# A graph layer with a gate on one core: more S1 T1 products split into quarters, and the order around them

## The chip, the cores and the metric

The kernel runs on one core of a Trainium2 chip. The metric is the device time of one execution in microseconds; the runs of the kernel before gave 1323.67, 1325.24 and 1325.05, median 1325.05. The profile is one further execution, with every engine's instructions recorded.

## The reference

1250 nodes with rows of 1024, 20000 edges (sorted by destination) of 8 types; everything is f32.

```python
h = maximum(layernorm(x), 0)
u = h @ root + bias
for r in range(8):                       # mean of the messages of type r, by destination
    sums = segment_sum(h[src] * (etype == r), dst); cnt = segment_sum(etype == r, dst)
    u = u + (sums / maximum(cnt, 1)) @ weight[r]
z = concatenate([u, h], 1) @ w_gate + b_gate
out = x + tanh(u) * z + h * (1 - z)
```

So there are eleven products of a 1250 x 1024 matrix with a 1024 x 1024 one: eight with `weight[r]`, one with `root`, and two with the halves of `w_gate`.

## The kernel before, in words

**Matrices and pairs.** The matrices are numbered s = 0 to 10 (`mats`, line 670): 0 to 7 are the types, 8 is `root`, 9 the half of `w_gate` that takes h, 10 the half that takes u. The kernel multiplies h by `weight[r]` first and gathers afterwards: row d of the result of type r goes to DRAM (`y`), and the edges fetch rows of it. The ten blocks of 128 nodes are taken as five *pairs* i = 0 to 4 (block i with block i + 5; NP = 5). `step(s, i)` does one pair of one matrix by `product`. The last matrix has a loop of its own at the end of the file.

**Strassen, once and twice.** `product` multiplies a pair (256 x 1024) by the matrix as 2 x 2 halves with seven products (the Strassen-Winograd form): A11 B11, A12 B21, S1 T1, S2 T2, S3 T3, S4 B22, A22 T4. Each is 4 matmuls of 512 columns for a pair, line 511; here it is called a *half-product*. For some of the seven, two neighbouring pairs (i = 0 and 1, or 2 and 3) are put together, so that the left side has two rows of blocks as well, and the half-products of both pairs are split once more, into quarters with seven products of 2 matmuls of 256 columns (line 255, `Second.add`): *quarter products*. Fourteen such matmuls stand in place of eight of 512 columns. The classes do this: `Second` for A12 B21, `Third` for S4 B22 (`thirds(s)`: s > EARLY = 3), `First` for A11 B11, `Fifth` for S1 T1. The fifth pair (i = 4) is the lone one: nothing is put together with it but the last half of work of others.

**Which pairs take S1 T1 by quarters** is told by `fifths(s, i)`, line 689: with FIFTHS = (1, 4) this is all pairs of s = 1 to 4 (where the lone pair only takes its bank from it) and the first two pairs of s = 5 to 9. Where it holds, `step` makes a `Fifth` at i = 0 or i = 2 and hands it to `product` as `root`; where it doesn't, `p5` does S1 T1 as a half-product (line 585) and copies it to the row (line 589).

**Banks.** PSUM has 8 banks here: a ring of four (`ps`, `bank()`), two of `ps_b` (`lead()`), one `ps_n` and one `ps_q`. While `fifths` holds, one bank of the ring is kept (`kept`, `sum_bank(1)`, line 134: a bf16 matmul of 512 columns, `touch`, writes it first), and the ring has three left. When a step begins for which `fifths` doesn't hold, the kept bank is let go.

**What else the engines do.** ACT copies banks to the rows and to scratch; DVE adds. In s = 1 to 4 DVE and POOL sort the edges into a table of slots. From s = 5 on the edges of the first five types are gathered beside the products: `edges` yields one *slot* at a time, which is one gather by POOL (line 1562, an indirect DMA of 128 rows of 4 KB into one of five buffers `got`) and one multiply-add on DVE (line 1567, 128 x 1024). In s = 8 and 9 the same is done for the last three types.

**Order.** All is written out by hand: each engine works in the order of the calls. `product` calls `between(j)` after each of its steps (through `done()`); there `step`'s `beside(j)` issues the additions that later products need (`q.sums()`, `first_sums()`, the differences of the next matrix's factors `make_t1` (line 195) and so on), and then the slots. `filled(name)` issues the quarter products that are put behind a step of `product`: a table `fill` in `step` says which. How many slots a call of `between` issues is told by `spread` (line 1620): each call adds a weight (10, 8, 13, 11, 8 for the five pairs) to a sum, and slots are issued up to that share of all. With a `root`, `product` makes one more call, `between(TICK)`, and leaves out that of `p5`.

For the steps of the change, these lines matter:

- `root.begin()` and `root.second()`, `root.late()`, `root.early()`: the quarter products of S1 T1, spread over `product`. They use `room` (scratch shared with `Third` and `First`), whose sums are on lines 309 to 312 (`sums`) and 315 to 318 (`next_sums`).
- Lines 424, 432, 434, 439, 445: ACT's and DVE's work on the banks of `Fifth`; 381, 383, 386, 391, 398: the same of `First`.
- Lines 261, 263, 267, 272: ACT's copies of the banks of `Second`; 282 and 283 (`to_first`), 289, 290 (`to_second`), 293: DVE's additions that read them. Line 283 frees a bank of the ring.
- Lines 537, 541, 543, 572, 589, 615, 659: copies and additions of `product` itself.

Of the kernel before, what the change touches and what calls it, by code (L numbers as in the profile page):

```python
# [21 lines left out]
def tile_rgcn_highway(  # L22
# [44 lines left out]
    NP = ND // 2  # L67
# [3 lines left out]
    R0 = (0, 5, R)  # L71
    K = ((28, 14, 13, 12, 11, 10, 9, 8, 7, 6), (20, 10, 8, 7, 7, 6, 5, 5, 4, 3))
    EARLY = 3
# [10 lines left out]
    TICK = 9  # L84
    LEFTS_AT = 6
    FIFTHS = (1, 4)
# [59 lines left out]
    def lead():  # L146

        return psum.tile([P, 512], F32, name="ps_b", bufs=2)
# [346 lines left out]
    def product(aop, w, to, between=lambda j: None, last=None, pieces=1, whole=True,  # L495
# [13 lines left out]
        def add(b, i, fresh=False, at=slice(0, Q), ks=range(KQ)):  # L509
            for k in ks:  # L510
                nc.tensor.matmul(b[:, at], aop[:, i, k, :], w.of[i][:, k, at],  # L511
                                 start=(fresh and k == 0), stop=(k == KQ - 1),
                                 skip_group_check=True)

        def done():
            between(step[0])
            step[0] += 1

        def filled(name):
            if fill and name in fill and fill[name]():  # L520
                done()
                return True
            return False
# [39 lines left out]
        def p1():  # L563
            if first is None:
                b = lead()
                add(b, A11, True)
            else:
                b = first.late() if head else first.to1
            if root and head:
                root.sums()  # L570
                first.fifth_to()
            nc.scalar.copy(c11, b)  # L572
            if root and head:
                root.second()
            done()
            filled("first")
            return b

        def p5(c=None):
# [14 lines left out]
        if root and head:  # L594
            root.begin()
            c = root.to0
            if inner:
                inner.c0 = c
            b = p1()
        elif first and head and early is None and "first" not in fill:  # L600
            c = inner.hold() if inner else sum_bank(odd) if narrow[0] else bank()
            add(c, S1, True, ks=range(KQ // 2))
            b = p1()
            p5(c)
        elif first and head:
            c = p5()
            b = p1()
        else:
            b = p1()
            if second:  # L610
                second()
                p2()
            c = p5()
# [74 lines left out]

    def fifths(s, i=0):

        return s >= FIFTHS[0] and (s <= FIFTHS[1] or i < 2)

    waiting, waiting_third, waiting_first, waiting_fifth = {}, {}, {}, {}
    at_call = [0, 0]
# [9 lines left out]
    def step(s, i, between=lambda j: None, second=None):  # L704

        two = paired(s, i)
        narrow[0] = fifths(s, i)
        if not narrow[0]:
            kept.clear()
# [6 lines left out]
        if two and i % 2 == 0:  # L716
            waiting[i] = Second(fac[s], i), t[0]
            if fifths(s, i):
                waiting_fifth[s, i] = Fifth(fac[s], i, room, p5_room)
# [13 lines left out]
        def beside(j):  # L733
# [28 lines left out]
            if (s, i, j) == (0, 0, 3) or (s > 0 and (i, j) == (3, int(thirds(s) or fifths(s)))):  # L762
                new.load_first()
# [205 lines left out]
    with ExitStack() as early:  # L969
# [20 lines left out]
        class Normed:  # L990
# [13 lines left out]
            def spread(self):  # L1004
                n = self.n
                nc.vector.bn_aggr(self.mv[:n], self.st[:n].rearrange("p a b -> p (a b)"))
                nc.scalar.activation(self.sd[:n], self.mv[:n, 1:2], AF.Sqrt, bias=eps[:n])
# [114 lines left out]
        first = ix1.tile([P, NCH], F32, name="first")  # L1122
# [394 lines left out]
        while going[0]:  # L1517
            s, i = next(steps)
# [11 lines left out]
    with ExitStack() as edges_part:  # L1530
# [89 lines left out]
        def spread(e, total, parts):  # L1620

            said = [0, 0]
            parts *= 10

            def between(j):
                said[0] += (10, 8, 13, 11, 8)[at_call[0]]
                while said[1] < min(total, -(-total * said[0] // parts)):
                    next(e, None)
                    said[1] += 1
                if said[0] == parts:  # L1630
                    for _ in e:
                        pass

            return between
# [36 lines left out]
        def beside(e, total, s, i, last):  # L1671


            between = spread(e, total, 7 * ((last - s) * NP + NP - i))
            while s <= last:
                step(s, i, between)
                s, i = next(steps, (NM, 0))
            return s, i

        s, i = next(steps)  # L1680
        while s <= EARLY:
            step(s, i)
            s, i = next(steps)
# [21 lines left out]
        class Passes:  # L1705
# [45 lines left out]
            def next(self):  # L1751
                nc.vector.tensor_single_scalar(self.done, self.done, float(-MORE), op=OP.add)
# [21 lines left out]
        while s < R0[1]:  # L1774
            step(s, i, on)
            s, i = next(steps)
# [14 lines left out]
        s, i = beside(first_group, sum(K[0]) + LATE + 1, s, i, R0[2] - 1)  # L1791
# [147 lines left out]
        while s < NM - 1:  # L1939
# [8 lines left out]
            s, i = next(steps, (NM, 0))  # L1948
# [86 lines left out]
```

## Time and profile before

| | |
|---|---|
| median of the runs shown | 1325.05 us |
| profiled execution, its own time | 1326.97 us |
| its span, first to last instruction | 1325.2 us |
| TensorE busy | 1310.1 us, 99% of the span |
| DVE busy | 1031.9 us, 78% |
| POOL busy | 637.4 us, 48% |
| ACT busy | 277.4 us, 21% |
| granted TensorE clock, mean | 0.998 |
| slots (line 1567) | 193, 1.28 us each |

The span is shorter than the execution's own time, which has 1.8 us around it. Each line of the profile is a group of instructions by source line, engine, operation, output and input; `x8` is the count. An f32 matmul is recorded as two instructions, so the count of a group is twice the program's. A busy share is an average over stages: here s = 0 to 4 work beside the sorting of the edges, s = 5 to 9 beside gathers, and s = 10 beside the gate. In the chain of work that ended last, each piece is named by its engine, output tile and line, and "issue" is time in which the engine waited for nothing that the profile shows.

### The profile page before, as it was taken

The numbers are of one execution on the slowest core, as the hardware profiler recorded it, in microseconds if no ns is written. First come the engines' busy times: TensorE is split into PE (matmuls) and PEld (weight loads), VectorE is DVE, ScalarE is ACT, GpSimd is POOL, SyncE is SP. The second block draws the span as 40 slices with busy tenths as digits, with TensorE's granted clock in tenths as the row PEclk, the third lists the DMA queues.
The fourth block names the chain that finished last, engine by engine and source line by source line (L and its number), as shares of the span: only waits on it lengthen the run. The fifth ranks groups of instructions, "written<-read, shape, count | busy, mean of one in ns | idle before, by whom it ended". The sixth has DMA issues, their size and how long they took to land.

```text
span 1325.2 us, 14354 instructions
## 1 busy us (share of the span) xinstructions
PE 1310.1 (99%) x4280; PEld 746.7 (56%) x4280; DVE 1031.9 (78%) x2171; ACT 277.4 (21%) x509; POOL 637.4 (48%) x981
## 2 busy tenths in 40 slices
PE   9999999999999999999999999999999999999997
PEld 5444565556465546555655665565565566544443
DVE  7768977797783676458987988897788799867974
ACT  3352111122112212211221211122121112222210
POOL 0001766666666675502453545356355556624632
PEclk9999999999999999999999999999999999999999
DMA  8976456762734242244748789888788967979961
GB/s 313 297 234 172 92 114 136 159 81 76 198 84 122 70 122 65 69 159 142 256 133 320 237 286 351 282 273 279 263 279 328 346 215 243 320 273 294 341 168 60
DMA packets 119397, 273.22 MB, mean 206 GB/s; under 512 B 33438, under 2 KB 45106, under 8 KB 119184
## 3 DMA queue, kind: packets, MB, share of 16 engines
q1 hardware_dynamic: 59120, 122.06, 30.7%
q0 software_dynamic: 44064, 118.20, 27.6%
q10 hardware_dynamic: 16128, 31.98, 7.8%
q8 instruction: 34, 0.56, 0.2%
q14 instruction: 51, 0.42, 0.1%
HBM read 210.73 MB, written 76.46 MB: 217 GB/s over the span
## 4 chain that ended last, share of the span: by engine, by line
PE 86%; issue 5%; DVE 3%; DMA 3%; POOL 2%; SPq 1%; ACT 0%; POOLq 0%; DVEq 0%; ACTq 0%
PE ps_b L511 41%; PE ps L255 19%; PE ps L511 11%; PE ps_b L255 4%; PE ps_n L511 3%; PE ps_n L255 3%; PE ps_q L255 2%; PE ps_q L511 2%; DMA xt<-in_x_dram 1%; DMA h_op<-z_dram,node 1%; DMA w<-in_L_gnn_weight_dram 1%; POOL out_dram L903 1%; POOL got L897 1%; DVE row L1959 0%; DVE h_op L1892 0%
## 5 line engine op out<-in xcount | busy, mean ns | idle before, releaser
L511 PE MATMUL ps_b<-w,h_op 128*128 128x512 f32 x1464 | 658.3, 594 | 1.0 <-ACT row L615 0.8
L511 PEld LDWEIGHTS ps_b<-w,h_op 128*128 128x128 f32 x1464 | 275.2, 190 | 301.2 <-issue 292.6
L1562 POOL DMA_INDIRECT got<-y,idx x193 | 249.2, 1291 | 284.5 <-DVE u L1567 182.9
L1567 DVE SCALAR_TENSOR_TENSOR u<-got,w_of,u 128x1024 f32<-128x1024 f32 (+1 forms) x193 | 246.9, 1282 | 37.1 <-DMA got<-y,idx 34.3
L1208 POOL DMA_INDIRECT table<-row_col,at_i x157 | 183.7, 1170 | 118.4 <-issue 85.2
L511 PE MATMUL ps<-w,h_op 128*128 128x512 f32 (+1 forms) x392 | 174.0, 586 | 0.2 <-DVE h_op L492 0.2
L511 PEld LDWEIGHTS ps<-w,h_op 128*128 128x128 f32 x392 | 73.6, 190 | 83.1 <-issue 78.9
L255 PE MATMUL ps<-inner 128*128 128x256 f32 x420 | 106.3, 380 | 0.0
L255 PEld LDWEIGHTS ps<-inner 128*128 128x128 f32 x420 | 79.2, 190 | 21.0 <-issue 9.6
L255 PE MATMUL ps<-w,h_op 128*128 128x256 f32 x340 | 88.3, 382 | 2.3 <-issue 1.3
L255 PEld LDWEIGHTS ps<-w,h_op 128*128 128x128 f32 x340 | 63.6, 190 | 31.0 <-issue 22.9
L537 ACT COPY row<-ps_b 128x512 f32<-128x512 f32 x53 | 31.0, 585 | 223.0 <-PE ps_b L511 213.6
L615 ACT COPY row<-ps_b 128x512 f32<-128x512 f32 x54 | 31.6, 585 | 215.5 <-PE ps_b L511 211.6
L511 PE MATMUL ps_n<-w,h_op 128*128 128x512 f32 x168 | 75.6, 593 | 0.0
L255 PE MATMUL ps<-w,w 128*128 128x256 f32 x288 | 70.6, 380 | 0.0
L255 PEld LDWEIGHTS ps<-w,w 128*128 128x128 f32 x288 | 54.4, 190 | 17.2 <-issue 11.0
L1216 POOL MEMSET apart<- 128x1 f32 x471 | 54.3, 115 | 18.1
L659 ACT COPY row<-ps_b 128x512 f32<-128x512 f32 x40 | 23.4, 584 | 185.1 <-PE ps_b L511 156.4
L543 DVE TENSOR_TENSOR row<-row 128x512 f32<-128x512 f32 x44 | 30.2, 686 | 39.1 <-ACT row L537 39.1
L1325 DVE SCALAR_TENSOR_TENSOR junk<-k_bc,key_col,before 128x128 f32<-128x128 int16 x157 | 55.0, 351 | 4.2
L511 PEld LDWEIGHTS ps_n<-w,h_op 128*128 128x128 f32 x168 | 31.7, 190 | 37.7 <-issue 37.1
L572 ACT COPY row<-ps_b 128x512 f32<-128x512 f32 x54 | 31.7, 587 | 84.0 <-PE ps_b L511 70.0
(257 smaller groups left out, 1568.9 us busy)
## 6 DMA issues: line engine op xcount, KB each, us to landing
y<-row SPq DMA_DIRECT2D x72, 512.0 KB
w<-in_L_gnn_weight_dram ACTq DMA_DIRECT2D x21, 1024.0 KB
w<-in_L_gnn_weight_dram SPq DMA_DIRECT2D x10, 1024.0 KB
w<-lefts_dram SPq DMA_DIRECT2D x16, 512.0 KB
w<-in_L_gnn_w_gate_dram ACTq DMA_DIRECT2D x6, 1024.0 KB
k_bc<-keys_dram SPq DMA_DIRECT2D x39, 128.0 KB
l_bc<-los_dram SPq DMA_DIRECT2D x39, 128.0 KB
h_dram<-h_op SPq DMA_DIRECT2D x9, 512.0 KB
```

What stands on the lines that cost most here:

```text
L255: nc.tensor.matmul(p, a[:, k, :], b[:, k, :], start=(fresh and k == 0), stop=(k == 1), skip_group_check=True)
L511: nc.tensor.matmul(b[:, at], aop[:, i, k, :], w.of[i][:, k, at], start=(fresh and k == 0), stop=(k == KQ - 1), skip_group_check=True)
L537: nc.scalar.copy(d, b)
L543: nc.vector.tensor_add(c22, c if lone else c22, d)
L572: nc.scalar.copy(c11, b)
L615: nc.scalar.copy(c12, b)
L659: nc.scalar.copy(c21, b)
L1208: ins = nc.gpsimd.indirect_dma_start(out=table[:, :], out_offset=bass.IndirectOffsetOnAxis(ap=at_i[:n, c:c + 1], axis=0), in_=row_col[:n, ...
L1216: nc.gpsimd.memset(apart, 0.0)
L1325: nc.vector.scalar_tensor_tensor(junk, o["k_bc"][:, i, :], key_col[:, c:c + 1], before, op0=OP.is_equal, op1=OP.mult, accum_out=rank[:, c: ...
L1562: nc.gpsimd.indirect_dma_start(out=t[:n], out_offset=None, in_=y[g][:, :], in_offset=bass.IndirectOffsetOnAxis(ap=at[:n, d, k:k + 1], axis=0),
L1567: nc.vector.scalar_tensor_tensor(u[:n], t[:n], w, u[:n], op0=OP.mult, op1=OP.add)
```

## The change

S1 T1 is taken by quarters in the first four pairs of s = 5, 6 and 7 as well (two pairs in s = 8 and 9 as before). In the lone pair of s = 4 `fifths` no longer holds: its S1 T1 goes to a bank of the ring, and the kept bank is let go there and taken again in s = 5. In `p1` of a second or fourth pair with both a `root` and an `inner` (s >= 4) the quarter products and additions of `fill["first"]` are issued ahead of the slots of that step. The extra call TICK counts for the slots at i = 0 alone, so that the number of slots by pair stays as it was.

```diff
@@ p1, in product
-            done()
-            filled("first")
+            if root and inner and not head:
+                filled("first")
+                done()
+            else:
+                done()
+                filled("first")
@@ fifths
-        return s >= FIFTHS[0] and (s <= FIFTHS[1] or i < 2)
+        return s >= FIFTHS[0] and (s <= EARLY or i < (NP - 1 if s < R0[2] else 2))
@@ between, in spread
-                said[0] += (10, 8, 13, 11, 8)[at_call[0]]
+                if j != TICK or at_call[0] == 0:
+                    said[0] += (10, 8, 13, 11, 8)[at_call[0]]
```

R0 = (0, 5, 8), so `s < R0[2]` is s < 8. With a `root` at i = 2, `step` takes another table `fill`, which was there for s = 4: the quarter products of `Second` move one place later, and its `seventh` with the additions of `to_first` goes from the third pair's end to the fourth pair's `first`.

## Prediction

> **What bounds the kernel now.** I read the engine totals first, then the chain of work that ended last, then the busy times by stretch with one stretch for each matrix.
>
> ```profile
> PE 1310.1 (99%) x4280; PEld 746.7 (56%) x4280; DVE 1031.9 (78%) x2171; ACT 277.4 (21%) x509; POOL 637.4 (48%) x981
> PE 86%; issue 5%; DVE 3%; DMA 3%; POOL 2%; SPq 1%; ACT 0%; POOLq 0%; DVEq 0%; ACTq 0%
> 693.06:808.30 115.24, 115.24 (x367) 68.80 (x367) 99.53 (x131) 22.03 (x45) 55.93 (x48) 1.00 0.81 279
> 808.30:923.44 115.14, 115.14 (x367) 68.80 (x367) 97.21 (x125) 22.02 (x45) 58.59 (x51) 1.00 0.85 298
> ```
>
> The first line is each engine's busy time and share, the second the chain by engine. In the other two the columns are PE, PEld, DVE, ACT and POOL busy time, granted clock, DMA share and GB/s. These are the stretches of s = 6 and s = 7 (measured from late in the fourth pair to the same point of the next matrix): TensorE is busy for the whole 115 us at full clock. So in these stages a matmul less is time less, as long as nobody makes TensorE wait. DVE has 16 to 18 us of idle time in each, which is the cover for what the change adds there.
>
> The chain inside s = 6, third and fourth pair, gives the price of a product:
>
> ```profile
> 775.42 3.43 PE ps_n L511 x8
> 778.85 0.86 PE ps L255 x4
> 779.72 1.85 PE ps_b L255 x8
> 781.56 1.73 PE ps L255 x8
> ...
> 787.59 3.51 PE ps_b L511 x8
> ...
> 800.58 3.43 PE ps L511 x8
> ...
> 807.44 0.86 PE ps L255 x4
> ```
>
> Each f32 matmul is two records, so x8 at L511 is one half-product (four matmuls of 512 columns): 3.43 us, 0.429 a record. At L255, x4 is one quarter product (two matmuls of 256 columns): 0.863 us, 0.216 a record. 775.42 and 800.58 are the S1 T1 of the third and of the fourth pair, the work that the change replaces. 1.85 in place of 1.73, and 3.51 in place of 3.43, is a matmul that waited about 0.1 us for an ACT copy.
>
> **What the order of instructions says.** Comparing the two programs engine by engine, POOL and SP issue the same instructions in the same order everywhere. TensorE, DVE and ACT differ inside s = 5, 6 and 7; outside, two DVE instructions of s = 4 stand behind the fourth pair's additions instead of ahead of them, and the lone pair's S1 T1 of s = 4 has another bank. TensorE issues 24 f32 matmuls of 512 columns less, 42 of 256 more, and one bf16 matmul of 512 columns more. DVE gets 18 additions of 256 and 12 of 512 columns more, ACT 6 copies of 256 and 3 of 512. So the case is three times the same edit, in the third and fourth pair of s = 5, 6, 7.
>
> **Part 1, S1 T1 by quarters.** Out: two half-products, 2 x 3.43 = 6.86 us a stage. In: seven quarter products, 7 x 0.863 = 6.04. Gain 0.82 a stage, 2.5 us in three. All of it is on the path, since TensorE has no gap there.
>
> [...]
>
> **Part 2, small waits.** In the third pair S3 now follows two quarter products after S2 and not one, so the 0.08 in 787.59 should go; in exchange the last quarter product waits for the broadcast copy at L439, as the one at L391 does in 779.72 (0.12). Net +0.04 a stage, 0.1 us in all; bounds -0.2 and +0.4.
>
> **Part 3, the bank that is kept.** It is let go in s = 4's lone pair, so it is taken and touched anew in s = 5: one more matmul of line 134.
>
> ```profile
> L134 PE MATMUL ps<-ident x5: 376/379/379, 153.1 to 1089.6; 128*128 128x512 bf16 x5
> ```
>
> It has the 379 ns (min/median/max of a record) of a 256-column f32 record, so its place in the stream costs 0.216 us. +0.2 us. The lone pair's product is the same work in another bank of the ring: nothing, unless that bank is late; no instruction of before shows such a wait (bounds 0 and 0.6, the largest gap of TensorE ahead of a product into `ps` between 130 and 520 us, at 453.5).
>
> **Part 4, DVE and ACT.** Ten DVE additions a pair: 6 x 0.34 + 4 x 0.60 = 4.4 us (spacings from the timeline: L311 to L312 0.34, L310 to L311 0.60). They fit: DVE was busy 34.55 of 42.40 us from 775.3 to 817.7. ACT has 1.3 us more in a stretch where it works 8.6. The cost is zero as long as what TensorE waits for comes in time, so I follow the queue through s = 6 with T = 775.42. TensorE: quarter products 0.863, half-products 3.43, in the order of the new program. DVE's queue as it starts:
>
> ```profile
> 775.05 6.43 DVE L1567 SCALAR_TENSOR_TENSOR u<-got,w_of,u 128x1024 f32<-128x1024 f32 x5
> 784.20 1.28 DVE L1567 SCALAR_TENSOR_TENSOR u<-got,w_of,u 128x1024 f32<-128x1024 f32 x1 [2.71 <-DMA got<-y,idx]
> ...
> 796.99 0.42 DVE L283 TENSOR_TENSOR row<-row,ps 128x256 f32<-128x256 f32 x1
> ```
>
> (A slot takes 1.31 us; the sixth waited 2.71 us for its gather.) After the change only one of those five slots stands ahead of the new sums; they need the earlier quarter products and end at 779.7. L398, three slots (3.9): 784.0. L434 needs the product that ends at 784.9, then L315 and L316 end at 786.3; TensorE wants them at 775.42 + 5 x 0.863 + 3.43 + 2 x 0.863 + 3.43 = 788.3. **Slack 2.0 us.** Then L317, L318, two slots, L445 (needs 790.9), L543, four sums: 794.1; six slots: 801.9; L282 and L283: 803.0. L283 frees the bank that the fourth pair's Second.second takes, at 788.3 + 6 x 0.863 + 3.43 + 2 x 0.863 = 798.7 (start of the fourth pair's additions) and + 5 x 0.863 + 3.43 = 806.4. **Slack 3.4 us**, where before it was 10 (797.4 against 807.44). That the fill stands ahead of the slots is worth one slot of it, 1.3 us. L316 of the fourth pair and L543 have over 4 us. So I cost DVE at nothing; what hides it is these slacks, and each us by which gathers make DVE later than 2.0 or 3.4 costs a us a stage. In the first pair the same queue, with some seven slots where the third has ten, ran in s = 6 to 9 with no wait of TensorE over 0.2 us.
>
> The slots' pace is unchanged: the extra call at i = 2 is left out of the count, seven counted calls remain.
>
> **Sum.** -2.5 + 0.1 + 0.2 = -2.2 us. The profiled execution took 1326.97 us (span 1325.2 and 1.8 around it): 1324.8. It lies 1.9 above the median of the three timed runs, 1325.05, on whose scale the forecast is **1322.85 us**, 0.17% less. About 0.2% (2.65 us, 1322.4) is what a measurement of this kernel can tell from no change, so the likeliest result is just under that.
>
> **Rivals.**
> 1. Slower: gathers ahead of L283. The six slots between the third pair's sums and L282 draw on five gather buffers that DVE now frees later, so the last of them can wait for its gather, L283 slips, and TensorE waits for the bank at the fourth pair's Second.second. For it: DVE waited 2.71, 2.2 and 1.9 us for gathers in these pairs of s = 6 and 7, once 4.4 in s = 8, at a DMA share of 0.85. Against: those waits came where DVE was early; s = 5 runs at 0.51. It decides from 3.4 us of lateness; to be slower by 2.65 us, each stage must lose (2.2 + 2.65)/3 = 1.6, that is lateness of 5.0. With one wait of 4.4 and one of 2.2 in each: 3 x (6.6 - 3.4) - 2.2 = +7.4, 1332.4. The same mechanism at a smaller size, a stall of 0.3 to 1.1 a stage, gives 1323.8 to 1326.2.
> 2. Faster: two idle pieces of s = 4 go.
>
> ```profile
> 531.44 1.30 issue
> ...
> 559.43 1.25 issue
> ```
>
> There TensorE waits for ACT copies (L272, L439) that came over a us after their product, with no queue ahead of them. If the moved additions or the other bank shift these, 2.6 us more: 1320.3. Against: the first lies in the second pair, before any DVE change, and TensorE's and ACT's orders are the same there.
> 3. It does what it says and the end does not move: from 1204 on the chain runs through the z gather (9.79 us), DVE and POOL. If that transfer is set by the gathers of the last group and not by TensorE, the gain is lost: 1325. Against: the piece ahead of the gather is TensorE's, without a gap back to s = 5.
>
> **How the numbers follow.** Forecast 0.60; rival 1 at full size 0.10, at the smaller size 0.12; rival 2 0.10; rival 3 0.08. Range: from rival 2 (1320.3) to the smaller stall (1326.2), which takes in the bounds of parts 2 and 3; left out are rival 1 at full size and the half of rival 2 that falls below, 0.15. Faster by over 0.2%: rival 2 and a bit under half of the forecast's cases, whose runs scatter by 0.8 us about 1322.85: 0.10 + 0.25 = 0.35. Within 0.2%: the rest of the forecast, rival 3 and the smaller stalls, 0.55. Slower 0.10.
>
> **What would show it.** Each of s = 5, 6, 7 takes 0.8 us less on TensorE and stays gapless: 114.1, 114.4, 114.3 in place of 114.88, 115.24, 115.14; s = 8 and later unchanged; DVE 4 to 5 us busier in each. Wrong if TensorE shows a wait ahead of a L255 product on `ps` in the third or fourth pair with DVE L283 or L316 as its releaser, or if the stages shrink and the end does not.

## The result and the profile after

| | before | after |
|---|---|---|
| median | 1324.13 us (1322.67 to 1325.24, 10 runs) | 1321.24 us (1320.60 to 1321.65, 10 runs) |
| ratio | 1 | 0.9978, interval 0.9970 to 0.9986 |
| profiled execution, own time (span) | 1326.97 (1325.2) | 1321.18 (1319.4) |

The runs of before are more here than the three known at the prediction, and their median is 0.9 us lower. The kernel is 0.22% faster; the forecast was 0.17%. That is just over the 0.2% up to which the prediction had put a chance of 0.55; the chance of more was 0.35.

The engines' totals and the chain of work that ended last, by engine, of the kernel after:

```profile
PE 1306.7 (99%) x4317; PEld 753.5 (57%) x4317; DVE 1045.5 (79%) x2201; ACT 281.3 (21%) x518; POOL 653.9 (50%) x981
PE 89%; issue 5%; DMA 2%; DVE 2%; POOL 2%; ACT 0%; POOLq 0%; DVEq 0%
```

TensorE has 37 records more and is busy 3.4 us less; DVE has 30 additions more and 13.6 us more of work. These totals hold every stage, so what the change did is read from the stretches. The stretches of s = 5, 6 and 7 after, cut at the same point of the program as before (columns: PE, PEld, DVE, ACT, POOL busy, granted clock, DMA share, GB/s):

```profile
574.41:688.70 114.29, 114.29 (x378) 71.07 (x378) 94.08 (x175) 23.25 (x48) 35.98 (x28) 1.00 0.51 170
688.70:803.11 114.41, 114.41 (x380) 71.09 (x379) 101.85 (x136) 23.25 (x48) 57.26 (x46) 1.00 0.81 280
803.11:917.40 114.29, 114.29 (x378) 71.07 (x378) 104.82 (x141) 23.25 (x48) 66.78 (x50) 1.00 0.85 299
```

114.88, 115.24 and 115.14 have become 114.29, 114.41 and 114.29: 0.59, 0.83 and 0.85 less, with TensorE still busy for all of each. s = 5 gives less because the new touch of the kept bank falls in it.

The chain in the third and fourth pair of s = 6, after:

```profile
775.50 3.43 PE ps_b L511 x8
778.93 1.73 PE ps L255 x8
780.66 3.43 PE ps_b L511 x8
784.09 0.86 PE ps L255 x4
784.96 0.86 PE ps_n L255 x4
785.82 2.65 PE ps L255 x12
...
789.34 3.43 PE ps_b L511 x8
...
798.81 3.43 PE ps_b L511 x8
802.24 0.86 PE ps L255 x4
```

The half-products of S1 T1 are gone, and quarter products stand between the others. In the third pair 775.50 is S2, 780.66 is S3 and 789.34 is A22 T4. S3 took 3.51 before and takes 3.43: its 0.08 us of waiting is gone. In exchange 2.65 in place of 2.59 holds the last quarter product's wait for ACT's copy, 0.06. From 784.09 on nothing waits for DVE; the DVE queue shows how near that was:

```profile
781.44 0.69 DVE L316 TENSOR_TENSOR inner<-w 128x512 f32<-128x512 f32 x1
...
789.67 6.55 DVE L1571 SCALAR_TENSOR_TENSOR u<-got,w_of,u 128x1024 f32<-128x1024 f32 x5
797.54 1.29 DVE L1571 SCALAR_TENSOR_TENSOR u<-got,w_of,u 128x1024 f32<-128x1024 f32 x1 [1.31 <-DMA got<-y,idx]
...
799.53 0.42 DVE L283 TENSOR_TENSOR row<-row,ps 128x256 f32<-128x256 f32 x1
```

(The slot's line 1567 is line 1571 in the kernel after.) L316 ends at 782.13, TensorE wants it at 784.09: 1.96 us to spare. L283 ends at 799.95, TensorE wants its bank at 802.24, for the fourth pair's `Second.second` (a quarter product): 2.29 to spare. The sixth slot waited 1.31 us for its gather.

**Where the 5.8 us between the two profiled executions are.** I cut both traces at ACT's copies of C11, the first block of a pair's result (line 572 of before, 576 of after; one for each pair of each matrix, early in the pair), and compared the lengths. Of s = 5, 6, 7 every stage has the same three differences, -2.57, +3.44 and -1.71 us, sum **-0.84** (the copy itself stands elsewhere in the two orders, so the single terms mean nothing). s = 5 has +0.25 more in its first pair, where the kept bank is touched. Together -2.52 + 0.25 = **-2.27 us** for the change. The pairs of s = 9 and 10 agree to 0.00. The rest is s = 4 with -3.40, the start of s = 8 with +0.27 and -0.4 at the very start: three waits of TensorE in s = 4 (1.46, 0.27 and 1.42 us of idle time at 531, 539 and 559) are in the profiled execution of before and not in that of after. Whether the change did that was the first question for the experiments.

### The profile page after: what moved, and what is told of

It is laid out like the page before. It is cut to its first block, busy times and chain, and to the rows that moved or that the text cites. A ratio compares the mean times of both kernels' runs of the same rounds, so it can differ in the third digit from the quotient of the medians.

```text
span 1319.4 us, 14482 instructions
## 1 busy us (share of the span) xinstructions
PE 1306.7 (99%) x4317; PEld 753.5 (57%) x4317; DVE 1045.5 (79%) x2201; ACT 281.3 (21%) x518; POOL 653.9 (50%) x981
## 4 chain that ended last, share of the span: by engine, by line
PE 89%; issue 5%; DMA 2%; DVE 2%; POOL 2%; ACT 0%; POOLq 0%; DVEq 0%
PE ps_b L511 43%; PE ps L255 19%; PE ps L511 11%; PE ps_b L255 4%; PE ps_n L255 4%; PE ps_n L511 3%; PE ps_q L255 2%; DMA got<-y,idx 2%; PE ps_q L511 2%; POOL out_dram L907 1%; POOL got L901 1%; PE ps L454 0%; PE ps_q L1254 0%; PE ps_q L1308 0%; DMA xt<-in_x_dram 0%
## 5 line engine op out<-in xcount | busy, mean ns | idle before, releaser
L511 PE MATMUL ps_b<-w,h_op 128*128 128x512 f32 x1464 | 658.0, 594 | 1.0 <-ACT row L619 0.8
L511 PEld LDWEIGHTS ps_b<-w,h_op 128*128 128x128 f32 x1464 | 275.5, 190 | 299.4 <-issue 291.0
L1566 POOL DMA_INDIRECT got<-y,idx x193 | 257.9, 1336 | 266.2 <-DVE u L1571 176.5
L511 PE MATMUL ps<-w,h_op 128*128 128x512 f32 (+1 forms) x368 | 163.2, 585 | 0.0
L255 PE MATMUL ps<-inner 128*128 128x256 f32 x456 | 114.9, 380 | 0.3 <-DVE inner L310 0.3
L511 PEld LDWEIGHTS ps<-w,h_op 128*128 128x128 f32 x368 | 69.0, 190 | 78.5 <-issue 75.2
L255 PEld LDWEIGHTS ps<-inner 128*128 128x128 f32 x456 | 86.1, 190 | 23.3 <-issue 9.6
L255 PE MATMUL ps<-w,h_op 128*128 128x256 f32 x352 | 91.2, 382 | 1.0 <-ACT w L272 1.0
L255 PEld LDWEIGHTS ps<-w,h_op 128*128 128x128 f32 x352 | 66.0, 190 | 30.9 <-issue 22.1
L255 PE MATMUL ps<-w,w 128*128 128x256 f32 x288 | 70.1, 380 | 0.0
L511 PE MATMUL ps_n<-w,h_op 128*128 128x512 f32 x144 | 64.8, 593 | 0.0
L255 PEld LDWEIGHTS ps<-w,w 128*128 128x128 f32 x288 | 54.4, 190 | 15.9 <-issue 9.6
```

What stands on the lines that cost most here:

```text
L255: nc.tensor.matmul(p, a[:, k, :], b[:, k, :], start=(fresh and k == 0), stop=(k == 1), skip_group_check=True)
L1566: nc.gpsimd.indirect_dma_start(out=t[:n], out_offset=None, in_=y[g][:, :], in_offset=bass.IndirectOffsetOnAxis(ap=at[:n, d, k:k + 1], axis=0),
```

## The experiments

Every ratio is to runs of the kernel before on the same chip at the same time. "By the pairs" is the comparison of lengths just described.

| kernel | median, us | ratio to before | interval |
|---|---|---|---|
| before again (b_again) | 1326.84 | 0.9995 | 0.9981 to 1.0009 |
| after again (a_again) | 1325.31 | 0.9981 | 0.9967 to 0.9995 |
| after, a third time (a_third) | 1322.28 | 0.9990 | 0.9981 to 0.9999 |
| bank alone (bank_alone) | 1328.73 | 1.0022 | 1.0011 to 1.0033 |
| bank alone again (bank_again) | 1323.70 | 1.0002 | 0.9993 to 1.0010 |
| moved additions alone (move_alone) | 1323.27 | 1.0001 | 0.9992 to 1.0010 |
| after without the moved additions (q_no_move) | 1327.84 | 1.0006 | 0.9992 to 1.0020 |
| quarters in s = 5 alone (q_s5_only) | 1323.12 | 0.9998 | 0.9989 to 1.0007 |
| after, more slots in the third pair (slots_17) | 1334.72 | 1.0094 | 1.0074 to 1.0114 |
| quarters up to s = 9 (q_all) | 1325.76 | 1.0017 | 1.0008 to 1.0026 |
| the same, slots evened (q_all_even) | 1327.09 | 1.0034 | 1.0022 to 1.0046 |
| quarters up to s = 8, slots earlier (q_to_8) | 1329.55 | 1.0001 | 0.9984 to 1.0019 |

My theory: 0.84 us less for each stage by the number of matmuls, 0.25 more once for the bank, no wait because DVE's two slacks hold; s = 4's waits are no part of the change. The rivals: the change acts through s = 4, or L283's lateness costs what the matmuls give.

### The two kernels again: are the waits of s = 4 the change's?

> The kernel before, unaltered, profiled once more. Theory: the change itself is worth 2.0 to 2.3 us (three stages of -0.84, +0.25 for the touch in s = 5, and +0.27 that comes back at the start of s = 8), and the 3.4 us by which the two profiled executions differ in s = 4 are a wait of that one execution, not of the kernel. Then this run's profile has less than 1 us of waits of TensorE in s = 4 and a span near 1322. Rival: s = 4 of the kernel before waits every time (the change took the waits away); then two waits of over 1.2 us, near 531 and 559 us, are here again and the span is 1324 or more.

> The changed kernel, unaltered, profiled once more. Theory: 2.0 to 2.9 us less than before in the median; s = 4 either free of waits or with such waits as any execution can have. Rival (s = 4 was cured by the change): no wait over 0.3 us in s = 4, and ratio 0.9975 or less.

> The changed kernel once more. Theory: 2.3 us less than before outside s = 4, ratio 0.9983, and in the profile every pair of s = 5 to 7 of the lengths of the first profile to 0.02 us; s = 4 and the start of s = 8 may differ by their waits, by 0 to 4 and 0 to 0.7 us. Rival (the waits of s = 4 are gone by the change): s = 4 without waits again.

All three are copies without an edit. In a_again s = 4 has waits of 2.18 and 1.93 us, more than the kernel before had. The chain of a_again in s = 4:

```profile
530.73 2.02 issue
...
558.21 1.98 PE ps_n L255 x4
```

Each of these two pieces holds an idle stretch of TensorE in place of a gapless hand-over. b_again has the first wait and not the second; a_third has none. From s = 5 on, a_again and a_third have the lengths of the first profile of after to 0.02 us but for the start of s = 8 (0.0 to 0.6 us). So the -3.40 us of s = 4 belong to the execution and not to the change, and the rival that s = 4 loses its waits by the change falls. The rest repeats to the hundredth, and 2.27 us is what the change does; the three ratios, 0.9978, 0.9981 and 0.9990, have the mean 0.9983, which of 1324 us is 2.3 us. (The third lies outside the interval of the first, so these intervals are too narrow for a comparison between series.)

The waits go by the series of runs. The experiments were run in four series, and the profiles of all four kernels of the first (b_again, a_again, bank_alone, q_no_move, on chip 3) have waits in s = 4, those of the seven kernels of the next two (chips 5 and 12) have none, and that of q_to_8, alone in the last (chip 5 again), has. The medians of before in these series are 1326.71, 1323.22, 1323.20 and 1329.10 us: where the profiles show the waits, the kernel before is slower too.

### One part alone: the bank, and the moved additions

bank_alone and bank_again are the kernel before with

```diff
-        return s >= FIFTHS[0] and (s <= FIFTHS[1] or i < 2)
+        return s >= FIFTHS[0] and (s <= EARLY or i < (NP - 1 if s <= FIFTHS[1] else 2))
```

> The kernel before with only the lone pair's bank changed: in s = 4 its S1 T1 goes to a bank of the ring, and the kept bank is taken and touched anew in s = 5. Theory: one matmul of line 134 more, +0.2 us, which is below what the timing tells (ratio 0.999 to 1.001), and s = 4 as in the kernel before. Rival: the kept bank was what s = 4 waited for; then this gives 1 to 3.4 us by itself.

> The kernel before with the lone pair's bank alone, once more. By its profile it costs 0.25 us (one bf16 matmul), ratio 1.0002. If its bank really costs what the five rounds showed, 1.0022 comes again, within its interval of 1.0011 to 1.0033; if that was the scatter of s = 4's waits, the interval holds 1.0002.

bank_alone's profile differs from before by the +0.25 us of the touch in s = 5, and by one wait less in s = 4, yet its runs gave 1.0022. The repeat on another chip gave 1.0002 with an interval that does not reach the first, and a profile with the same +0.25 and no waits in s = 4. The repeat fits the 0.25 us; the first ratio is not explained by any row. Its series is the first, in which the runs of before lie between 1324.63 and 1332.74 us; in that of the repeat they lie between 1322.55 and 1324.51. A ratio of one series can so be off by 0.2% here, as much as the whole change, and its interval does not tell.

move_alone is the kernel before with the edit of `p1`:

```diff
-            done()
-            filled("first")
+            if root and inner and not head:
+                filled("first")
+                done()
+            else:
+                done()
+                filled("first")
```

> The kernel before with the fourth pair's additions ahead of the slots alone, which without the quarters moves two DVE additions of s = 4 only. Theory: nothing, ratio 1.0000 within its interval, every pair from s = 5 on as before. Rival (the moved additions of s = 4 are what takes the waits of s = 4 away): s = 4 3.4 us shorter, ratio 0.9975.

1.0001, and every pair from s = 5 on as before, but for 0.07 at the start of s = 8. Without the quarters the move does nothing. (Its s = 4 has no waits in the profiled execution; those of before's are 3.4 us, and the ratio shows that this is not the move's work.)

### One part undone: the additions behind the slots again

q_no_move is the kernel after with

```diff
-            if root and inner and not head:
-                filled("first")
-                done()
-            else:
-                done()
-                filled("first")
+            done()
+            filled("first")
```

> The change without its moved additions: in the second and fourth pair the slots stand ahead of the first fill again, as before. Theory: DVE's L283 comes one slot (1.3 us) later, which is inside the 2.3 us that it was early in the changed kernel (799.9 against 802.2), so the time is that of the changed kernel within 0.5 us. Rival: the moved additions carry the gain; then TensorE waits ahead of the fourth pair's Second.second by 0.5 to 1.5 us a stage, 1.5 to 4.5 us in all, and the gain is gone.

By the pairs s = 6's fourth pair is 1.40 us longer than in the kernel after, and s = 5 and 7 are as there; s = 4 has 5.9 us more, in waits of the kind just told and, after the second, 1.7 us at half the clock (last section). The expectation, to stay within half a us, missed. DVE's queue of q_no_move in s = 6 (its slot is line 1567):

```profile
795.43 6.56 DVE L1567 SCALAR_TENSOR_TENSOR u<-got,w_of,u 128x1024 f32<-128x1024 f32 x5
803.17 1.29 DVE L1567 SCALAR_TENSOR_TENSOR u<-got,w_of,u 128x1024 f32<-128x1024 f32 x1 [1.19 <-DMA got<-y,idx]
806.75 1.29 DVE L1567 SCALAR_TENSOR_TENSOR u<-got,w_of,u 128x1024 f32<-128x1024 f32 x1 [2.29 <-DMA got<-y,idx]
...
808.74 0.42 DVE L283 TENSOR_TENSOR row<-row,ps 128x256 f32<-128x256 f32 x1
```

and the chain of q_no_move there:

```profile
799.19 7.47 DMA got<-y,idx
...
808.74 0.43 DVE row L283
809.17 0.04 issue
809.22 1.13 PE ps L255 x4
```

Seven slots stand ahead of L283 where the kernel after has six. The seventh has no buffer ahead of it: its gather, issued only when the first buffers came free, took 7.47 us, and DVE stood still for 2.29 us. Against the kernel after that is 1.3 us for the slot and 2.2 more of waiting (1.19 + 2.29 against 1.31), 3.5 in all, with a slack of 2.29: L283 ends late, and TensorE waits 1.2 us. This is rival 1 of the prediction, at its place and by its mechanism. The moved additions, which by themselves do nothing, keep it away in s = 6. In s = 7 seven slots stand there too, but the sixth and the seventh wait 0.93 and 1.12 us, and L283 ends at 923.45 where TensorE wants it at 923.54: all the slack is used and nothing is lost.

### More slots ahead of L283

slots_17 is the kernel after with

```diff
-                    said[0] += (10, 8, 13, 11, 8)[at_call[0]]
+                    said[0] += (10, 8, 17, 11, 4)[at_call[0]]
```

> The changed kernel with other shares of slots (10, 8, 17, 11, 4): one slot more ahead of the third pair's L434 and two more between the third pair's sums and L282, L283; the orders of TensorE, ACT and POOL are those of the changed kernel. Theory (L283's slack is what hides DVE): the slack measured in the changed kernel's s = 6 is 2.3 us, and two slots are 2.6 us of DVE besides the gathers' waits, so TensorE waits 0.3 to 3 us a stage at the fourth pair's Second.second, released by DVE L283, 1 to 9 us in all. Rival (DVE's place is no matter as long as its total work is the same): the time of the changed kernel within 0.3 us outside s = 4.

1.0094, and by the pairs 11.4 us more than the kernel after in its profiled execution, of which 1.94 in s = 6 and 5.12 in s = 7. The theory covers these two. The rest is in s = 8 and 9, where the slots were moved too and TensorE waits for other instructions: 2.3 us for L316 and 1.8 for an ACT copy (L333), none for L283. DVE's work is the same (1046.8 us busy, 1045.5 in the kernel after): it is only done in another order. DVE's queue in s = 7 and TensorE's beside it:

```profile
905.85 6.57 DVE L1571 SCALAR_TENSOR_TENSOR u<-got,w_of,u 128x1024 f32<-128x1024 f32 x5
916.59 3.90 DVE L1571 SCALAR_TENSOR_TENSOR u<-got,w_of,u 128x1024 f32<-128x1024 f32 x3 [4.17 <-DMA got<-y,idx]
...
921.19 0.42 DVE L283 TENSOR_TENSOR row<-row,ps 128x256 f32<-128x256 f32 x1
```

```profile
914.84 3.60 PE L511 MATMUL ps_b<-w,h_op 128*128 128x512 f32 x8
921.67 1.13 PE L255 MATMUL ps<-w,h_op 128*128 128x256 f32 x4 [3.24 <-DVE row L283]
922.63 5.29 PE L511 MATMUL ps_b<-w,h_op 128*128 128x512 f32 x8
```

Eight slots in place of six. The first five follow each other without a wait; the sixth waits 4.17 us. TensorE stands 3.24 us at the fourth pair's Second.second, and the releaser is named: L283. In s = 6 the sum from the rows of after is 2.6 (two slots) + 1.4 (gathers waited 2.69 us there, 1.31 in after) - 2.29 (slack) = 1.7; the pair grew by 1.94. So one us of lateness beyond the slack is about one us of time. In s = 7 it is more than that: 5.12 for a wait of 3.24, mostly because the half-product after the wait took 5.29 and not 3.60. That is told below. s = 5, where the DMA share is 0.51, has no wait at all: its eight slots follow each other in 10.53 us, and L283 ends 1 us ahead of TensorE (686.86 against 687.84).

### One stage alone, and two stages more

q_s5_only has the quarters of four pairs in s = 5 alone:

```diff
-        return s >= FIFTHS[0] and (s <= EARLY or i < (NP - 1 if s < R0[2] else 2))
+        return s >= FIFTHS[0] and (s <= EARLY or i < (NP - 1 if s <= R0[1] else 2))
```

> The quarters of S1 T1 in the first four pairs of s = 5 alone; s = 6 and 7 take them in two pairs as before; everything else as in the changed kernel. Theory (0.84 us for each stage that takes quarters, plus 0.25 us once for the kept bank): 0.84 - 0.25 = 0.6 us less than before outside s = 4, ratio about 0.9996; in the profile only s = 5 is 0.84 us shorter, and the pairs of s = 6 and 7 have the lengths of before to 0.1 us. Rival (the gain is no matter of the stages but of the changed order at the end of s = 4): the whole 1.7 us less remains.

By the pairs: -0.84 and +0.26 in s = 5, s = 6 and 7 as before to 0.00. The ratio, 0.9998, holds -0.6 us and could not tell it from nothing; the profile can.

q_all has them in all stages:

```diff
-        return s >= FIFTHS[0] and (s <= EARLY or i < (NP - 1 if s < R0[2] else 2))
+        return s >= FIFTHS[0] and (s <= EARLY or i < NP - 1)
```

> The same as the changed kernel, and the first four pairs of s = 8 and 9 take S1 T1 by quarters too. Theory of the matmul count: two more stages at 0.84 us each, 1.7 us less than the changed kernel, about 4.0 us less than before outside s = 4, ratio about 0.997. Rival (gathers ahead of L283, where DVE waited 4.4 us for a gather in s = 8): TensorE waits at the fourth pair's Second.second in s = 8, 1 to 5 us, with DVE L283 as its releaser, and the time is that of the changed kernel or above it.

1.0017, and by the pairs s = 8 and 9 take 3.6 us more than in the kernel after, not 1.7 less. What TensorE waited for in s = 8 and 9 of q_all (us in total, times, longest):

```profile
PE ps L255 <- DVE inner L316: 2.4, 2, 1.8
PE ps L255 <- DVE row L283: 1.5, 2, 1.0
PE ps L255 <- DVE inner L310: 0.7, 1, 0.7
```

L283 is late for the fourth pair's Second.second in both, with seven slots ahead of it and a wait of 3.37 us for a gather in s = 8. But more is lost at L316 in s = 9, late in the first pair and ahead of the third, where no slot waits for a gather. By its busy time DVE is just full there (no run tried it with less work): in the first two pairs of s = 9 it is busy in 48.48 of 49 us (47.70 in the kernel after).

q_all_even has fewer slots ahead of L283 there; its `w` is (9, 9, 10, 10, 12) in s = 8 and 9:

```diff
-                    said[0] += (10, 8, 13, 11, 8)[at_call[0]]
+                    said[0] += w[at_call[0]]
```

> Quarters in the first four pairs of s = 5 to 9, as in the kernel with all stages, and the shares of slots of s = 8 and 9 changed from 10, 8, 13, 11, 8 to 9, 9, 10, 10, 12: five slots instead of seven stand between the third pair's sums and L282, L283, and one less ahead of the third pair's L434. Theory (the order of DVE is what took the gain of s = 8 and 9): the waits at the fourth pair's Second.second, 1.18 us in s = 8 and 0.69 in s = 9, go, so that it comes out about 2 us below the kernel with all stages; the two waits for L316 in s = 9 (1.8 and 0.8 us) stay unless a slot less happens to stand ahead of them, and the lone pair's extra slots may cost up to 1 us at the start of s = 9; against the changed kernel between 1 us less and 2 us more. Rival (the gathers set the pace and what is not late at L283 is late elsewhere): the same time as the kernel with all stages, 2.5 us above the changed one.

1.0034. What TensorE waited for in s = 8 and 9 of q_all_even:

```profile
PE ps L255 <- DVE inner L316: 2.9, 3, 1.9
PE ps L255 <- DVE inner L310: 2.0, 2, 1.1
```

The waits for L283 are gone, and s = 8 from its second pair on gives the -0.84 us of the others, so there the theory of the order holds. But with more slots in the lone pair of s = 8, L310 is late there and in the first pair of s = 9 (1.1 us each at most), L316 is late in s = 9 as before, and from that lone pair to the end of s = 9 it takes 5.5 us more than the kernel after. The rival was right about the sum.

q_to_8 leaves s = 9 alone and puts slots of s = 8 into its first pairs (`w` is (12, 9, 10, 11, 8) there):

```diff
-        return s >= FIFTHS[0] and (s <= EARLY or i < (NP - 1 if s < R0[2] else 2))
+        return s >= FIFTHS[0] and (s <= EARLY or i < (NP - 1 if s <= R0[2] else 2))
...
-                    said[0] += (10, 8, 13, 11, 8)[at_call[0]]
+                    said[0] += (w if said[0] < 350 else (10, 8, 13, 11, 8))[at_call[0]]
```

> The changed kernel with the quarters in the first four pairs of s = 8 too (s = 9 as it is), and the slots of s = 8 shared as 12, 9, 10, 11, 8, so that five and not seven stand between its third pair's sums and L282, L283, with none put into the lone pair. Theory: s = 8 takes 0.84 us less than in the changed kernel, with no wait of TensorE at L283 or L316 in its third and fourth pair; the rest as in the changed kernel, so 0.8 us below it outside s = 4 and the start of s = 8 (ratio to before about 0.9975). Rival (slots taken ahead of the first pair's additions make those late in their turn): a wait of 0.5 to 2 us in the first or second pair of s = 8, released by DVE L310 or L316, and the time of the changed kernel or above it.

The same view of q_to_8, s = 8 and 9:

```profile
PE ps L255 <- DVE inner L310: 2.7, 2, 2.1
PE ps L255 <- DVE inner L316: 2.2, 2, 1.2
```

Again the third and fourth pair of s = 8 keep their gain and the additions ahead of them are late instead, as the rival had it: s = 8 takes 3.3 us more than in the kernel after, s = 9 1.3. (Its s = 4 is 4.7 us longer too, by the waits told above and the half clock after one of them.) The ratio, 1.0001, is from runs that scatter by 6 us against runs of before that scatter by 8.5, so the pairs carry this. No version that beat the kernel after was found: in s = 8 and 9 each sharing of the slots moved the wait to another addition.

## Why the prediction was right

The time was within the range and the mechanism was the forecast's. By its steps:

- **What bounds the kernel.** TensorE without gaps in s = 5 to 9, so that a matmul less is time less: confirmed, and the end moved by the whole sum (s = 9 and 10 are equal to 0.00), so rival 3 (the end does not move) falls.
- **Part 1**, -0.82 a stage, and **part 2**, +0.04: together -0.78 forecast, -0.84 measured. Of the small waits, the 0.08 at S3 went as said; the one at the last quarter product is 0.06 and not 0.12, so part 2 is -0.02 a stage and not +0.04. The new records cost what the old ones did: the 1792 at L255 in the trace after are 0.216 us apart in the median, as the 1708 before (1.5 ns over half of the 0.429 of L511), and the sum of three stages is -2.52 us.
- **Part 3**, the touch, +0.2: measured 0.25 to 0.26 in each kernel that has it. In the list of what would show it I left it out of s = 5, so 114.1 there should have read 114.3; 114.29 came.
- **Part 4**, DVE at nothing: right in s = 5 to 7. The slack at L316 was 2.0 and is 1.96. At L283 it was 3.4 and is 2.29: the step that failed in size is that six slots follow each other without a wait; the sixth waited 1.31 us for its gather, which the first rival had named and the sum had not taken in. That each us later costs a us a stage held in s = 6 of the kernel with more slots and fell short in s = 7, where the clock added 1.7. That it cost nothing was near: one slot more uses all of the slack (q_no_move, s = 6 and 7).
- **DVE's busy time** was forecast to grow by 4 to 5 us in each stage. Over the whole run it grew by 13.6, which is 4.5 for each of the three; in the single stretches it was 1.4, 2.3 and 7.6, since they are cut by TensorE and DVE's instructions fall on other sides of the cuts (8, 5 and 16 more of them where 10 were added to each).
- **The moved fill** was costed as one slot, 1.3 us. It is worth more: a slot and the wait for the gather behind it, and without it the change loses 1.4 of its 2.3 us, all of it in s = 6.
- **Rival 1** was real and near, at 2.29 us of slack. It did not happen in the kernel after, and it does with one slot more (q_no_move, in s = 6 alone), two more (slots_17, in s = 6 and 7) or in the next two stages (q_all).
- **Rival 2**: the two idle pieces of s = 4 did go in the first profile, but not by the change; the reason against it held.
- **The scale.** The forecast was 1322.85 on a median of three runs of before; of ten runs it was 1324.13, 0.92 lower, which is over half of the 1.6 us between forecast and result. The rest, 0.7 us, is no part of the sum: by the pairs the change is 2.27 us, as forecast. It is of the size of the scatter between the ratios, and no run shows more of it. That the result still lay in the range owes something to luck: the low end, 1320.3, came from rival 2, and the change did not do what rival 2 said.

**What stays open**: what makes the waits of s = 4 come in some series, and why bank_alone's first ratio was 1.0022.

## What to carry to other kernels

Where one engine has no gaps, trade its work by its records' prices, but look then for the instruction of the other engine that frees a buffer for it, and compute when it ends: "16 us idle in this stage" said nothing, and 2.3 us at one addition decided. Count what stands ahead of that instruction in pieces that have their data and pieces that have not: in s = 6 and 7, at a DMA share of 0.81 to 0.85, the first five slots cost 1.3 us each, and the ones after them up to a gather's wait more (the sixth 0.69 to 4.17 us); in s = 5, at 0.51, eight ran without a wait. When two profiled executions differ by more than the edit explains, cut both at the same instructions and repeat them before you give the difference a cause.

## What the runs showed of the hardware

**Waits that belong to the execution.** In s = 4, while POOL issues short indirect transfers (30 from 505 to 565 us; their queue moved 0.30 MB there, before as after), TensorE waits for ACT's copies 0 to 4.1 us in all, in either kernel, though ACT has nothing ahead of them (in the kernel before it was idle for 0.87 us ahead of L272 and for 1.53 ahead of L439); with the half clock told below s = 4 is up to 5.9 us longer. The profiled executions fall in two kinds, told apart by the DMA share from 505 to 565 us. The kernel after first, then a_again, the same program:

```profile
505.00:565.00 60.00, 60.00 (x216) 40.15 (x215) 31.61 (x68) 14.46 (x31) 34.62 (x35) 1.00 0.32 54
```

```profile
505.00:565.00 60.00, 56.21 (x203) 37.64 (x202) 30.95 (x68) 13.70 (x29) 35.37 (x36) 1.00 0.19 53
```

The share is 0.28 to 0.32 in the eight executions without waits and 0.19 to 0.21 in the six with them, with about as many bytes moved (51 to 57 GB/s). In q_to_8, one of the six, the chain goes through 2.96 us that the trace can put down to no engine of this core. They come by the series of runs, as told above. I did not find the cause, and no experiment was made on it.

**Half the clock after a short idle piece.** After the 3.24 us of waiting in s = 7 of slots_17, the granted clock was about half, 0.52 over 3.2 us, and not at once. Windows of slots_17: the idle piece, then from 1.5 us after its end, then later (the clock is third from the end):

```profile
918.00:921.50 3.50, 0.43 (x2) 0.00 (x0) 3.33 (x4) 0.58 (x1) 3.05 (x3) 1.00 1.02 410
923.20:926.40 3.20, 3.20 (x5) 1.35 (x4) 3.20 (x6) 0.00 (x0) 2.71 (x2) 0.52 1.03 413
927.00:930.00 3.00, 3.00 (x14) 2.26 (x13) 2.93 (x3) 0.59 (x1) 1.55 (x1) 1.00 1.04 384
```

Records of 512 columns were 0.853 us apart there in place of 0.429; the eight of the half-product took 5.13 us of the chain in place of 3.43, and the loss is 1.7 us on top of the wait. The same came after idle pieces of 2.9 us (q_to_8) and 2.3 us (q_no_move) in s = 4, from 1.1 to 1.4 us after TensorE was at work again, with the same loss; it did not come after those of 2.3 (q_to_8, in s = 8) and 2.2 us (a_again). (These lengths are counted from start to start of two records, less the usual 0.216; the idle time in the profile is 0.16 us less, 2.8, 2.1, 2.1 and 2.0. The 3.24 is such an idle time.) The half clock of q_to_8 and of q_no_move:

```profile
535.10:538.50 3.40, 3.40 (x5) 1.33 (x4) 2.35 (x5) 0.00 (x0) 0.00 (x0) 0.50 0.01 0
```

```profile
562.20:565.20 3.00, 3.00 (x8) 2.36 (x7) 2.98 (x8) 0.37 (x1) 0.95 (x1) 0.50 0.00 0
```

After 2.3 us of idle time the half clock came once and once not, and where it came, TensorE had been busy again for 1.1 to 1.5 us. Of the four idle pieces of 2.3 us or more that the traces have between 130 and 1200 us, three cost 1.7 us more than themselves; why the fourth did not is not shown.
